# Weight sums of a context-cluster block moved along GpSimd's queue, one half of a norm handed to ScalarE, and the filler pieces of the last batch dealt out anew

## The chip, the cores and the metric

The kernel runs on one core of one Trainium2 chip. A core has TensorE (PE: matmuls, with its weight loads on PEld), VectorE (DVE), ScalarE (ACT), GpSimd (POOL) and the SP queue, which issues most DMAs. Each engine works through its own instructions in the order in which the program issues them. The metric is the device time of one execution in microseconds (us). Before the change the median of three runs is 3128.08 us (3124.45 to 3131.26).

## The reference

Two layers act on x of shape (4, 256, 64, 64), all in float32. The first is full self-attention over the 4096 pixels of an image. The second is a context-cluster block: a norm, two 1x1 convolutions f and v, similarity of every pixel to four centres of its region and head, the best centre taken, sums by centre given back to the pixels, a projection, a residual; then a second norm, an MLP with gelu, another residual, and a scaled pointwise convolution with relus.

```python
q, k, v = (1x1 convolutions of x)                  # q, k: 32 channels, v: 256
x = gamma * softmax(q k) v + x                     # attention, each image
feat, val = conv1x1(gn1(x), f_w, f_b), conv1x1(gn1(x), v_w, v_b)   # 96 channels
sim = sigmoid(beta + alpha * cn . pn)              # unit centres . unit points
sim = sim * one_hot(argmax(sim, axis=centres))
agg = (sim @ v2 + v_cen) / (mask.sum() + 1)
y = x + ls1 * conv1x1(sim.T @ agg, proj_w, proj_b)
hdn = conv1x1(gelu(conv1x1(gn2(y), mlp_w1, mlp_b1)), mlp_w2, mlp_b2)
y = y + ls2 * hdn
z = relu(bn(y * dw_w)); z = relu(bn(conv1x1(z, pw_w)))
```

## The kernel before

The four images are taken one after the other (loop over `b`, L2056). For each there are three stages. **Weighting** (L958) is the attention: 64 units of 4x128 keys by 512 queries, each with score products (L489), the subtraction of the maximum (L655), exponentials (L659 to L661) and the weighted sum (L734). Products of 2x2 blocks are done with seven multiplications instead of eight, so sums of operands have to be made beforehand; GpSimd makes most of them (L664). **Cluster** (L1140) is the first norm, the products of f and v (L1331), the similarities, the choice of the best centre and the projection back. **MLP** (L1634) is the second norm and the MLP, again with seven products, whose weights have to be summed too.

The order of all instructions is written out by hand (`manual_schedule`, L2052), and so is the filling of TensorE's gaps: `fill(n)` (L2044) takes matmuls of a list until their sizes reach n. For the images 0, 1 and 2 the list holds the v, q and k projections of the next image (L443, L351). Image 3 has no next one; its list holds the last 512-pixel block of image 2, which was kept back (`late_block`, L1518). Its pieces are numbered here 0 to 36: 0 to 15 are `first` (L1549), 16 to 31 `second` (L1566; each image column c ends with an ACT instruction L1575, a GpSimd addition L1576, an ACT relu L1577, and after c = 1 a GpSimd subtraction L1586), 32 is empty, 33 to 36 are `last` (L1592, with relus L1600).

What the change touches:

- `turn_mlp` (L248) and `turn_w2` (L1622) make weight sums on GpSimd: L251, L252, L1627, L1629, L1631, each 128x512. For the images 0 to 2 `turn` (L2075) issues all five, for image 3 only the three of `turn_w2`; there `turn_mlp` runs at the end of the weighting (L1087). The cluster stage calls `turn` at L1398, after the choice of the best centres in the program; but on GpSimd's own queue the instruction in front is the last square of `heads` (L1308), so that is what they follow.
- The f and v loop (L1319) runs over eight blocks. Each has 16 matmul records, two additions out of PSUM (L1341), two of the similarities (L1350), a square on GpSimd (`heads`, L1310) and a sum over it on VectorE (L1312). PSUM for it has two buffers (`ps_s`).
- After the loop comes the tail of the choice on VectorE: affine (L1268), `largest` (L1273 to L1281), `weights` (L1286), for two halves in turn, then the sums on TensorE (`summed`, L1366), counts (L1401), transposes (L1412, L1421) and the projection (L1434), then the products with the pixels (L1456).
- `group_norm` (L301) is mean and variance by bn_stats, two matmuls with `left` and `avg` (L309, L310), another (L320), ACT's square root (L224), a reciprocal (L226), and scale and offset (L326, L327). For the second norm it has `meanwhile` load gelu's table right behind the square root. Then `norm(0, nc.vector)` (L1745) applies scale and offset to two channel halves of block 0 (L1667) and makes the sums of it (L1734 to L1737), all on VectorE; the first two hidden products (L1854) need them, and the ACT copy L1862 comes behind the first product.
- At the very start, while no score of the first query block is weighted yet (`alone`, L865), the generator `load_rest` (L176) issues weight loads a part at a time, one part for every u above 2. Its last part is no load but the first sums of `wpw_s` on GpSimd (L188, L189). Behind it on GpSimd stand `added(5)`, `added(6)`, the first `factors` and `added(7)` (L664 all).

Of the kernel before, what the change touches and what calls it, by code (L numbers as in the profile page):

```python
# [10 lines left out]
AF = mybir.ActivationFunctionType  # L11
ALU = mybir.AluOpType
# [48 lines left out]
def attention_then_cluster_block(  # L61
# [17 lines left out]
    nc = tc.nc  # L79
# [168 lines left out]
    def turn_mlp():  # L248

        _, w_cd, _, w_d = own_w["q"]  # L250
        nc.gpsimd.tensor_tensor(w_cd, w_cd, w_d, ALU.add)  # L251
        nc.gpsimd.tensor_scalar(w_d, w_d, -1.0, None, ALU.mult)  # L252

    def roots():
        for s, v in ((dw_d, "dw_v"), (pw_s, "pw_v")):
# [41 lines left out]
    def table(f):  # L297

        nc.scalar.activation(probe, probe, f)
# [30 lines left out]
    def block(tiles, k, nb):  # L330
        o = (nb % 2) * NB
        return tiles[nb // 2][:, k, o : o + NB]
# [5 lines left out]
    def attention(b, xs, ys):  # L338
# [526 lines left out]
        def alone():  # L865

            roots()
            for i in range(2):
                v_pair(i)
            k0, q0 = staged()  # L870
            for i in range(2, 5):
                v_pair(i)

            def added(*gs):
                for g in gs:
                    for f in sums(g):
                        f()

            added(0, 1)
            rest = load_rest()  # L880
            for u in range(GRP):
                half(u, 0)()
                if u < GRP - 1:
                    half(u, 1)()
                else:

                    sc = products(u, 1)
                    highest_of(0, tiles(sc))
                    kept(u, 1, sc)
                if u == 0:  # L890
                    k1 = halved("k", 1, False)
                    for i in range(4, GRP):
                        k_straight(i, k1)
                elif u == 1:
                    q1 = halved("q", 1, False)
                else:
                    v_pair(u + 3)
                    if u % 2 == 0:
                        added(u // 2 + 1)
                if 1 < u < 6:  # L900
                    written("kqkq"[u - 2], (u - 2) // 2, *(k0, q0, k1, q1)[u - 2], nc.gpsimd)
                if u == 3:
                    q_block(1)
                    k_unit(GRP)
                if u > 2:
                    next(rest, None)
            fold(0)
            v_pair(11)
            added(5)
            tp = turned_over(0, ps_m.tile([P, 4, P], F32, tag="m", name=f"tt_{b}_0"))  # L910
            half(GRP, 0)
            v_pair(12)
            dgs["dg"] = across(0, "w2", tp)
            v_pair(13)
            added(6)
            spread(0, dgs["dg"])
            v_pair(14)
            wf()
            exps(0)
            factors(0)  # L920
            v_pair(15)
            half(GRP, 1, True)
            added(7)
            for _ in rest:
                pass
# [32 lines left out]
        def weighting(next_x, fill, early, begin):  # L958
# [23 lines left out]
            for u in range(units):  # L982
                nb, g = divmod(u, GRP)
# [99 lines left out]
            nb = NBLK - 1  # L1083
            for _ in range(4):
                next(quarters)
            if b == B - 1:
                turn_mlp()  # L1087
            table(AF.Sqrt)
            ends = b == B - 1
            fill(1 if ends else 2)  # L1090
# [23 lines left out]
                    stop=True,  # L1114
                )
            nc.scalar.copy(rdens[nb], inv)
            fill(6 if ends else 7)
            t = ts[nb].rearrange("p (h k) n -> p h k n", h=2)
            nc.vector.tensor_tensor(t, t, over(nb), ALU.mult)
            add_one(nb)  # L1120
# [19 lines left out]
    def cluster(b, ys, stats, cells, rest, fill, gelu, nxt, maxima, turn):  # L1140
# [161 lines left out]
        def heads(nb, between=lambda: None):  # L1302
# [13 lines left out]
                ALU.add,  # L1316
            )

        for nb in range(NBLK):  # L1319
            fh, o = nb // 4, nb % 4  # L1320
            if 1 < nb + 1 < NBLK:
                norm(nb + 1)
            if nb in later:
                later[nb]()
            xn = xns.pop(nb)

            ps = ps_s.tile([P, 2, 2, C], F32, tag="s", name=f"fv_{b}_{nb}")
            for j in range(4):
                g = j // 2
                for k in range(KC):  # L1330
                    nc.tensor.matmul(  # L1331
                        ps[:, g, j % 2, : 2 * ED + 16],
                        xn[:, k, j * P : (j + 1) * P],
                        mix[:, k, fh, 16 * g : 16 * g + 2 * ED + 16],
                        start=(k == 0),
                        stop=(k == KC - 1),
                    )
            if nb == NBLK - 1:
                heads(nb - 1)
            for g in range(2):  # L1340
                nc.vector.tensor_tensor(  # L1341
                    vf[nb // 2][:, nb % 2, 2 * g : 2 * g + 2, :],
                    ps[:, g, :, 16 - 16 * g : 16 - 16 * g + 2 * ED],
                    fvb.unsqueeze(1).to_broadcast([P, 2, 2 * ED]),
                    ALU.add,
                )
            for g in range(2):
                q = 2 * fh + g
                d0 = 2 * ED * g
                nc.vector.tensor_tensor(  # L1350
                    folded(sgs[fh])[:, g, 2 * o : 2 * o + 2],
                    ps[:, g, :, d0 : d0 + 16],
                    dot_b[:, q * 16 : (q + 1) * 16].unsqueeze(1).to_broadcast([P, 2, 16]),
                    ALU.add,
                )
            if 0 < nb < NBLK - 1:
                heads(nb - 1)
            if nxt and nb == 2:
                nxt.queries()

        agg_p = ps_a.tile([P, NB], F32, tag="a0", name=f"agg_{b}")

        def summed(w, first):
# [19 lines left out]
        fill(0 if nxt else 2)  # L1383
        summed(lambda j, q: pool_w[:, j], True)
        gelu(1)
        fill(5 if nxt else 4)
        table(AF.Sqrt)
        for _ in best:
            pass
# [5 lines left out]
        summed(lambda j, q: sim[:, j, q, :], False)  # L1395
        count(0)
        count(1)
        turn()  # L1398

        cnt_p = ps_a.tile([P, NB], F32, tag="a1", name=f"cnt_{b}")  # L1400
        nc.tensor.matmul(cnt_p[:ED, :64], ones[:, :ED], bests[0], start=True, stop=True)  # L1401
# [99 lines left out]
        seen(1, 0)  # L1501
        seen(1, 1)
        if not nxt:
            fill(6)
            return stats2

        nxt.q_block(0)
# [111 lines left out]
        t = own_w["w2"]  # L1619
        return t[:, :h_n, :P], t[:, h_n:, :P], t[:, :h_n, P:], t[:, h_n:, P:]  # L1620

    def turn_w2(b, kept):  # L1622


        a11, _, a21, a22 = quarters_w2()
        w7 = work.tile([P, h_n, P], F32, tag="rden", bufs=1, name=f"w2_7_{b}")
        nc.gpsimd.tensor_tensor(w7, a21, a11, ALU.subtract)  # L1627
        s1 = work.tile([P, h_n, P], F32, tag="q", name=f"w2_1_{b}") if kept else a21
        nc.gpsimd.tensor_tensor(s1, a21, a22, ALU.subtract)  # L1629
        s2 = work.tile([P, h_n, P], F32, tag="q", name=f"w2_2_{b}")  # L1630
        nc.gpsimd.tensor_tensor(s2, s1, a11, ALU.subtract)  # L1631
        return s1, s2, w7

    def mlp(b, ys, stats2, fill, nxt, blocks, turned, maxima):  # L1634

# [14 lines left out]
        few = swap.tile([P, h_n + 3, P], F32, tag="mix", name=f"w2_3_{b}")  # L1650
        w3_s, (pw_bcd, pw_bac, pw_abcd) = few[:, :h_n], (few[:, h_n + i] for i in range(3))
        nc.gpsimd.tensor_tensor(w3_s, s2_s, a12_s, ALU.add)
        ga, gb = group_norm(
            b, "gn2", stats2, fill, meanwhile=lambda: table(AF.Gelu_apprx_tanh)
        )
        ob = out[b].rearrange("(k p) h w -> p k (h w)", p=P)
        pairs = {}

# [2 lines left out]
        def norm(nb, eng):  # L1661


            pairs[nb] = pr = spool.tile([P, 2, KC, NB], F32, tag="s", name=f"xn2_{b}_{nb}")

            def scaled(k):
                nc.vector.tensor_scalar(  # L1667
                    pr[:, 0, k, :],
                    block(ys, k, nb),
                    ga[:, k : k + 1],  # L1670
                    gb[:, k : k + 1],
                    ALU.mult,
                    ALU.add,
                )

            def parts():
                rest = factors(eng, pr[:, 0], pr[:, 1])
                scaled(0)
                if nb == 0:
                    next(rest)  # L1680
                scaled(1)
                yield
                yield from rest

            rest = parts()
            next(rest)
            return rest
# [56 lines left out]

        for _ in norm(0, nc.vector):  # L1745
            pass

        def product(out, w, j, x):
            nc.tensor.matmul(out, w[:, j * P : (j + 1) * P], x, start=True, stop=True)
# [302 lines left out]
    with tc.manual_schedule():  # L2052
        here = attention(0, xs0, [])
        here.alone()
        late = None
        for b in range(B):  # L2056
            xs1 = []
            nxt = attention(b + 1, xs1, []) if b + 1 < B else None

            def next_x():  # L2060
                if nxt:
                    xs1.append(load_x(b + 1, len(xs1)))

            begin, todo, gelu = late or (
                lambda: None,
                list(nxt.projections) if nxt else [],
                lambda i: None,
            )
            fill = filler(todo)
            stats, cells, rest = here.weighting(  # L2070
                next_x, fill, [] if b else derived(), begin
            )
            turned = []

            def turn():  # L2075
                if nxt:
                    turn_mlp()
                turned.extend(turn_w2(b, not nxt))

            maxima = []  # L2080
            stats2 = cluster(b, here.ys, stats, cells, rest, fill, gelu, nxt, maxima, turn)

            late = mlp(b, here.ys, stats2, fill, nxt, NBLK - (b == B - 2), turned, maxima)
            here = nxt
# [76 lines left out]
```

## Time and profile before

| | us |
|---|---|
| median of 3 runs | 3128.08 |
| lowest, highest | 3124.45, 3131.26 |
| the profiled execution, whole | 3132.96 |
| its span, first to last instruction | 3131.2 |
| PE busy | 3052.7 (97%) |
| DVE busy | 2513.3 (80%) |
| GpSimd (POOL) busy | 2330.7 (74%) |
| ACT busy | 1780.1 (57%) |
| mean granted TensorE clock | 0.994 |

A line of the timeline reads: start, duration, engine, line of the kernel, operation, output tile <- input tiles, shapes, count, and in brackets the idle time of that engine before it with what ended it. The windows view gives, for each stretch, its length, the busy time of every engine with its number of instructions, the granted TensorE clock (1.00 is full), and the share and rate of the DMA engines. PE's 97% is a mean: in 80 us windows most of the weighting and MLP stages lie at 99% and more, the windows around the cluster stage at 91 to 94% (73.30 of 80 us from 560 to 640, 75.42 from 1280 to 1360, 73.56 from 2080 to 2160, 73.05 from 2880 to 2960).

### The profile page before, as it was taken

Reading aid. Unit: us, or ns where it says so; the run is one execution under the profiler, and the core shown is the slowest. Engines: PE = TensorE matmul, PEld = TensorE weight load, DVE = VectorE, ACT = ScalarE, POOL = GpSimd, SP = SyncE. Lnnn points to the kernel's source line nnn. Section 1 sums busy time; section 2 is a strip of 40 time slices with the busy share of each in tenths; the row PEclk is TensorE's granted clock in tenths of the full one; section 3 lists DMA queues with packets and bytes.
Section 4 is the critical chain, followed back from the end, with each engine's and each line's share of the span. In section 5 each row is a group of like instructions: output and inputs, shape, how many; then the busy total and the mean of one; then the engine's idle time right before and its main releaser. Section 6 shows DMA issues by size and latency. Waiting matters only on the chain.

```text
span 3131.2 us, 41360 instructions
## 1 busy us (share of the span) xinstructions
PE 3052.7 (97%) x14210; PEld 2498.0 (80%) x14210; DVE 2513.3 (80%) x3548; ACT 1780.1 (57%) x2817; POOL 2330.7 (74%) x2243
## 2 busy tenths in 40 slices
PE   8999999999999999999999999999999999999999
PEld 5788887788688888878868888886877888875886
DVE  4999888777798888877779888877768988887675
ACT  5666664544566666454556666645446666655444
POOL 5888886477588888657758888955766988893563
PEclk9999999999999999999999999999999999999999
DMA  5112226100112113510011212440011112150000
GB/s 174 47 56 64 61 90 168 58 18 28 48 47 68 55 61 111 157 44 26 19 58 44 68 61 64 117 144 34 28 41 44 59 57 67 55 153 1 14 21 28
DMA packets 105570, 200.40 MB, mean 64 GB/s; under 512 B 14880, under 2 KB 30864, under 8 KB 103824
## 3 DMA queue, kind: packets, MB, share of 16 engines
q1 hardware_dynamic: 100464, 178.66, 17.9%
q0 software_dynamic: 4256, 18.90, 2.9%
q8 instruction: 113, 1.85, 0.2%
q14 instruction: 97, 0.79, 0.1%
q10 hardware_dynamic: 640, 0.20, 0.0%
HBM read 147.01 MB, written 48.34 MB: 62 GB/s over the span
## 4 chain that ended last, share of the span: by engine, by line
PE 73%; DVE 9%; POOL 9%; issue 3%; ACT 3%; DMA 2%; SPq 1%; POOLq 0%; ACTq 0%; DVEq 0%
PE av L734 34%; PE mo L1771 10%; PE sc L489 7%; PE hq L1854 5%; PE hp L1854 3%; PE hr L1854 3%; PE fv L1331 3%; POOL acc L664 3%; POOL t L664 2%; DVE top L513 2%; DVE s L655 2%; PE vp L443 2%; POOL s L664 1%; PE mo L1755 1%; PE hq_pw L1854 1%
## 5 line engine op out<-in xcount | busy, mean ns | idle before, releaser
L502 ACT COPY s<-sc 128x1024 f32<-128x1024 f32 x512 | 515.2, 1012 | 426.3 <-PE sc L489 418.2
L655 DVE TENSOR_TENSOR s<-s,hold 128x1024 f32<-128x1024 f32 x512 | 598.5, 1209 | 9.9 <-ACT hold L638 6.0
L664 POOL TENSOR_TENSOR acc<-acc,t 128x512 f32<-128x512 f32 x408 | 541.9, 1348 | 0.0
L734 PE MATMUL av<-s,sum 128*128 128x256 f32 x2048 | 527.1, 380 | 5.5 <-POOL s L664 5.3
L734 PE MATMUL av<-t,v 128*128 128x256 f32 x2048 | 527.2, 380 | 2.5 <-POOL t L664 2.4
L734 PE MATMUL av<-s,v 128*128 128x256 f32 x2048 | 525.7, 379 | 2.5 <-ACT t L764 1.3
L664 POOL TENSOR_TENSOR s<-t,s 128x512 f32<-128x512 f32 x256 | 341.9, 1336 | 221.9 <-DVE t L678 154.9
L678 DVE TENSOR_TENSOR t<-s,hold 128x1024 f32<-128x1024 f32 x256 | 311.7, 1217 | 189.4 <-POOL acc L664 98.1
L513 DVE TENSOR_TENSOR top<-sc,top 128x1024 f32<-128x1024 f32 x350 | 426.6, 1219 | 21.4 <-ACT s L502 17.6
L734 PEld LDWEIGHTS av<-s,v 128*128 128x128 f32 x2048 | 387.3, 189 | 65.0 <-ACT xn L1722 2.3
L734 PEld LDWEIGHTS av<-s,sum 128*128 128x128 f32 x2048 | 387.7, 190 | 63.7 <-POOL s L664 11.4
L734 PEld LDWEIGHTS av<-t,v 128*128 128x128 f32 x2048 | 387.4, 190 | 63.4 <-POOL t L664 8.9
L1809 ACT ACTIVATE hs<-hs,pv_s 128x256 f32<-128x256 f32 x496 | 232.6, 503 | 353.2 <-DVE hs L1845 353.2
L489 PE MATMUL sc<-q,k 128*128 128x512 f32 x1024 | 392.8, 468 | 20.0 <-ACT s L502 9.6
L1771 PE MATMUL mo<-hs,w 128*128 128x256 f32 x1512 | 385.0, 381 | 0.0
L664 POOL TENSOR_TENSOR t<-s 128x512 f32<-128x512 f32 x256 | 330.3, 1290 | 45.4 <-PE av L734 31.8
L1771 PEld LDWEIGHTS mo<-hs,w 128*128 128x128 f32 x1512 | 283.7, 190 | 47.3 <-ACT hs L1809 6.2
L659 ACT ACTIVATE hold<-s 128x512 f32<-128x512 f32 x256 | 154.2, 602 | 214.9 <-DVE s L655 214.7
L1845 DVE TENSOR_TENSOR hs<-hq,hs 128x256 f32<-128x256 f32 x496 | 198.5, 421 | 86.6 <-PE hq L1854 76.2
L661 ACT ACTIVATE s<-s 128x1024 f32<-128x1024 f32 x256 | 266.9, 1043 | 0.0
L734 PE MATMUL av<-t,sum 128*128 128x256 f32 x1024 | 262.4, 378 | 0.0
L489 PEld LDWEIGHTS sc<-q,k 128*128 128x128 f32 x1024 | 174.2, 189 | 108.2 <-DVE top L513 59.1
(292 smaller groups left out, 4878.5 us busy)
## 6 DMA issues: line engine op xcount, KB each, us to landing
k<-k SPq DMA_DIRECT2D x248, 256.0 KB, 2.7
x<-in_x SPq DMA_DIRECT2D x62, 512.0 KB, 6.9
out<-xn SPq DMA_DIRECT2D x62, 256.0 KB, 2.1
att<-t SPq DMA_DIRECT2D x56, 256.0 KB, 4.0
x<-att POOLq DMA_DIRECT2D x12, 1024.0 KB, 9.9
w<-in_w SPq DMA_DIRECT2D x8, 1024.0 KB, 11.8
q<-q SPq DMA_DIRECT2D x31, 256.0 KB, 4.1
rden<-row_rd SPq DMA_DIRECT2D x28, 256.0 KB, 3.7
```

The source lines that it names most:

```text
L489: nc.tensor.matmul(sc[:, r, :], k_s[:, (2 * h + r) * P : (2 * h + r + 1) * P], qs[u // GRP], start=True, stop=True,)
L502: nc.scalar.copy(slots[u][:, PAIR[h]].rearrange("p h r n -> p r h n"), tiles(sc))
L513: nc.vector.tensor_tensor(top, src, top if saved[nb] is None else saved[nb], ALU.max)
L655: nc.vector.tensor_tensor(sh, sh, mb.to_broadcast([P, 2, 2, QW]), ALU.subtract)
L661: nc.scalar.activation(s[:, PAIR[1]], s[:, PAIR[1]], AF.Exp)
L664: nc.gpsimd.tensor_tensor(out, x, y, op)
L678: nc.vector.tensor_tensor(t31[u], s[:, B11 : B22 + 1 : 2], b12.to_broadcast([P, 2, 2, QW]), ALU.add)
L734: nc.tensor.matmul(av[bank][:, half_ * QW : (half_ + 1) * QW], a[:, r], t[:, r], start=(g == 0 and r == 0 and i in (1, 7, 2, 4)), stop=(g ...
L1771: return nc.tensor.matmul(bank[:, half * HB : (half + 1) * HB], a[:, j], t, start=start, stop=stop)
L1809: nc.scalar.activation(src, src, AF.Gelu_apprx_tanh, bias=pvc("b1", P, j + 4 * (i > 1)))
L1845: nc.vector.tensor_tensor(dst, ps, term, ALU.add)
L1854: nc.tensor.matmul(out, w, x, start=True, stop=True)
```

## The change

Five edits, none of which changes an operand or a result's formula.

1. `turn_mlp` and `turn_w2` become generators. `turn` is started before the f and v loop, one instruction of it is issued after each `heads(nb - 1)` of the blocks 1 to 6, and what may be left is issued after the loop; the call behind the choice goes.
2. The second norm no longer loads gelu's table behind the square root; the table is loaded after `norm(0)`. In `norm(0)` the second channel half is made by ACT (Identity with scale and offset) instead of VectorE.
3. The `wpw_s` sums of the start are not issued at u = 7; they come with the rest of `load_rest`, behind `added(7)`.
4. In image 3 the pieces of the kept block are handed out otherwise: 8 instead of 6 at the end of the weighting, 6 instead of 4 after gelu(1), 2 instead of 6 after the products with the pixels. So 2 pieces come earlier from there up to the f and v loop, and 4 fewer are left for the wait before the second norm.
5. `turn_mlp` at the end of image 3's weighting is run through at once, as before.

```diff
     def turn_mlp():
         _, w_cd, _, w_d = own_w["q"]
-        nc.gpsimd.tensor_tensor(w_cd, w_cd, w_d, ALU.add)
-        nc.gpsimd.tensor_scalar(w_d, w_d, -1.0, None, ALU.mult)
+        yield nc.gpsimd.tensor_tensor(w_cd, w_cd, w_d, ALU.add)
+        yield nc.gpsimd.tensor_scalar(w_d, w_d, -1.0, None, ALU.mult)
...
-                if u > 2:
-                    next(rest, None)
+                if 2 < u < 7:
+                    next(rest)
...
             if b == B - 1:
-                turn_mlp()
+                for _ in turn_mlp():
+                    pass
...
-            fill(6 if ends else 7)
+            fill(8 if ends else 7)
...
+        turning = turn()
         for nb in range(NBLK):
...
             if 0 < nb < NBLK - 1:
                 heads(nb - 1)
+                next(turning, None)
...
+        for _ in turning:
+            pass
...
-        fill(5 if nxt else 4)
+        fill(5 if nxt else 6)
...
         count(1)
-        turn()
...
         if not nxt:
-            fill(6)
+            fill(2)
             return stats2
...
-    def turn_w2(b, kept):
+    def turn_w2(b, kept, turned):
...
-        nc.gpsimd.tensor_tensor(w7, a21, a11, ALU.subtract)
+        yield nc.gpsimd.tensor_tensor(w7, a21, a11, ALU.subtract)
...
-        nc.gpsimd.tensor_tensor(s1, a21, a22, ALU.subtract)
+        yield nc.gpsimd.tensor_tensor(s1, a21, a22, ALU.subtract)
...
-        nc.gpsimd.tensor_tensor(s2, s1, a11, ALU.subtract)
-        return s1, s2, w7
+        yield nc.gpsimd.tensor_tensor(s2, s1, a11, ALU.subtract)
+        turned.extend((s1, s2, w7))
...
-        ga, gb = group_norm(
-            b, "gn2", stats2, fill, meanwhile=lambda: table(AF.Gelu_apprx_tanh)
-        )
+        ga, gb = group_norm(b, "gn2", stats2, fill)
...
             def scaled(k):
-                nc.vector.tensor_scalar(
-                    pr[:, 0, k, :],
...
-                )
+                dst, src = pr[:, 0, k, :], block(ys, k, nb)
+                a, s = ga[:, k : k + 1], gb[:, k : k + 1]
+                if nb == 0 and k:
+                    nc.scalar.activation(dst, src, AF.Identity, scale=a, bias=s)
+                else:
+                    nc.vector.tensor_scalar(dst, src, a, s, ALU.mult, ALU.add)
...
         for _ in norm(0, nc.vector):
             pass
+        table(AF.Gelu_apprx_tanh)
...
             def turn():
                 if nxt:
-                    turn_mlp()
-                turned.extend(turn_w2(b, not nxt))
+                    yield from turn_mlp()
+                yield from turn_w2(b, not nxt, turned)
```

More of the change, by code (lines that the diff above doesn't have):

```diff
@@ L1666, in scaled @@
             def scaled(k):
-                nc.vector.tensor_scalar(
-                    pr[:, 0, k, :],
[L1669 to L1673, printed above, removed]
-                )
+                dst, src = pr[:, 0, k, :], block(ys, k, nb)
[4 more added lines that the diff above has]
+                    nc.vector.tensor_scalar(dst, src, a, s, ALU.mult, ALU.add)
             def parts():
```

## The prediction

> **What bounds the kernel now.** First the page's chain: which engine holds the end.
>
> ```profile
> PE 73%; DVE 9%; POOL 9%; issue 3%; ACT 3%; DMA 2%; SPq 1%; POOLq 0%; ACTq 0%; DVEq 0%
> ```
>
> TensorE is the bound, and an edit pays only where the chain leaves it. The chain in order of time leaves it in the cluster stage of each image and in the first 90 us. So I read the timeline there; this is image 0 just after f and v:
>
> ```profile
> 565.93 1.33 POOL L251 TENSOR_TENSOR w<-w 128x512 f32<-128x512 f32 x1
> 568.88 1.26 POOL L1627 TENSOR_TENSOR w<-w 128x512 f32<-128x512 f32 x1
> 569.29 1.14 DVE L1281 TENSOR_TENSOR scr<-scr 128x256 f32<-128x256 f32 x1
> 570.22 1.34 POOL L1629 TENSOR_TENSOR w<-w 128x512 f32<-128x512 f32 x1
> 570.46 1.38 DVE L1286 TENSOR_TENSOR sim<-sg,scr 128x256 f32<-128x256 f32 x1
> 571.64 1.32 POOL L1631 TENSOR_TENSOR w<-w 128x512 f32<-128x512 f32 x1
> 571.76 1.49 DVE L1268 TENSOR_SCALAR sg<-sg 128x256 f32<-128x256 f32 x1
> 575.11 0.42 DVE L1281 TENSOR_TENSOR scr<-scr 128x256 f32<-128x256 f32 x1
> 575.57 0.43 DVE L1286 TENSOR_TENSOR sim<-sg,scr 128x256 f32<-128x256 f32 x1
> 576.05 2.78 PE L1366 MATMUL agg<-vf,sim 128*32 128x96 f32 x60 [3.71 <-DVE sim L1286]
> ```
>
> The reader sees the same VectorE instructions twice: beside GpSimd's weight sums each ends 0.2 to 0.3 us after a GpSimd sum ends, and without one it takes a third of that. PE idles 3.71 us behind them. The windows view shows what comes of it (the column before the last two is the granted clock):
>
> ```profile
> 572.00:574.00 2.00, 0.34 (x5) 0.13 (x4) 1.93 (x3) 1.29 (x2) 1.24 (x3) 1.00 0.04 8
> 574.00:576.00 2.00, 0.00 (x0) 0.00 (x0) 1.86 (x6) 0.00 (x0) 0.00 (x0) 0.65 0.00 0
> 576.00:578.00 2.00, 1.95 (x52) 1.95 (x56) 0.98 (x2) 0.00 (x0) 0.00 (x0) 0.50 0.00 0
> 578.00:580.00 2.00, 2.00 (x27) 1.71 (x18) 0.59 (x2) 0.24 (x1) 0.00 (x0) 0.50 0.00 0
> ```
>
> After the gap TensorE runs at half clock. Image 3, where the gap is shorter, does the same sums in 1.51 us at full clock, but loses its clock at another gap, before the first norm:
>
> ```profile
> 2826.00 0.38 PE L309 MATMUL gnm_gn<-mv_gn,left 128*128 128x1 f32 x2 [1.92 <-DVE mv_gn L307]
> 2865.21 0.28 DVE L1268 TENSOR_SCALAR sg<-sg 128x256 f32<-128x256 f32 x1
> 2868.29 1.51 PE L1366 MATMUL agg<-vf,sim 128*32 128x96 f32 x60 [1.41 <-DVE sim L1286]
> ```
>
> At the start GpSimd waits for a weight that nobody needs yet, and VectorE later waits for GpSimd:
>
> ```profile
> 58.62 0.46 POOL L188 TENSOR_TENSOR wpw_s<-wpw_s 128x128 f32<-128x128 f32 x1 [8.05 <-DMA wpw_s<-in_wpw]
> 79.59 1.22 DVE L678 TENSOR_TENSOR t<-s,hold 128x1024 f32<-128x1024 f32 x1 [5.24 <-POOL acc L664]
> ```
>
> **Edit 1, the sums moved into f and v, images 0 to 2.** On the chain L1275 goes from 0.51 to 0.43 us, L1281 from 1.15 to 0.44, L1286 from 1.38 to 0.44, L1268 from 1.42 to 0.21 (0.28 busy less overlap, image 3): -2.94. So the 60 matmuls start at 573.1. PE's last work before ends at 572.35, so 0.76 us of idle time stay, and all 2.94 count. With so short a gap the clock should stay. From these matmuls to the projection (L1434) image 3 takes 2868.29 to 2871.71, 3.42 us at full clock; image 0 took 576.05 to 581.83, 5.78; image 1 1350.34 to 1356.38, 6.04; image 2 2123.18 to 2128.04, 4.86. The clock gives 2.36 + 2.62 + 1.44 = 6.4, the shorter chain 3 x 2.94 = 8.8: **-15.2**. Behind it everything (matmuls, k loads that wait for PE, VectorE's statistics) hangs on PE and moves along.
>
> The cover in the loop: PE needs 2.81 us a block.
>
> ```profile
> 546.53 0.83 POOL L1310 TENSOR_TENSOR vf<-vf 128x384 f32<-128x384 f32 x1 [1.92 <-DVE vf L1341]
> 546.57 0.54 DVE L1312 TENSOR_REDUCE prn<-vf 128x16 f32<-128x384 f32 x1
> ```
>
> GpSimd idles 1.92 to 2.05 us between squares and a sum takes 1.26 to 1.81, so the next square is not late. VectorE's loop work is 1.02 + 0.28 + 0.54 = 1.84 of 2.81. Its additions read PSUM and one tile; a like one, L655, ran its usual 1.2 us beside GpSimd sums, and the row above shows the reduce unharmed by a square. Cost 0; bounds 0 and, if a sum delays an eviction by its whole 1.33, 0.36 a block (1.84 + 1.33 - 2.81) x 13 sums = 4.7. The weights are there: image 1's load lands at 1298, the loop starts at 1314.
>
> By "TensorE: Matmul & The Clock Gate" of the Trainium skill (Part 1) the clock halves after an idle window of about 3.4 us: 0.76 us keeps it, as I assume, but the 1.92 us gap above should have kept it too, and the trace halves it; by the page the 1.35 us claimed below for image 3 would be nothing.
>
> **Edit 3, the start.** GpSimd is idle from 50.57 to 58.62. Freed, `added(5)` (four of 0.81) runs from 52.4, when its v copy is there; `added(6)` waits for the copy ending at 57.17 and ends at 60.4. Then the first s sum waits for L678, at 63.4 instead of 65.94. The rows to `added(7)`'s end took 9.8 us, collisions included; with 1.05 for the moved L188 and L189, the second unit's s sum starts at 74.2 instead of 75.71; one collision less (0.3) makes -1.8. The chain goes on over L678 at 79.59 to PE at 89, and PE has 1.19 + 0.20 + 0.59 + 0.21 + 1.47 + 0.33 = 4.0 us of gaps there. **-1.8**, bounds 0 and -4.0.
>
> **Edit 2, second norm, images 0 to 2.** VectorE sheds L1667, 0.47. But ACT must first copy v out (L451), which waits for PE: in image 1 to 1378.1. An Identity of this shape takes 0.81 (L1529), so L1735 starts at 1378.9 instead of 1378.81; image 0 0.28 later, image 2 0.07: **+0.4**; bounds -1.4 (all of L1667 three times) and +1.7, when L451's 0.57 comes on top each time. Table load and probe (1.28 + 0.20) now stand before the copy L1862: 1380.26 instead of 1380.09, hidden, since the third PSUM bank's user starts after 1381.2.
>
> "ScalarE: Activation LUTs" (What ACT_TABLE_LOAD costs) puts a switch at 2.66 us with its drain; the rows show 1.28 and the probe right behind. By the page L1862 ends 1.4 us late, some 1.2 us beyond that cover, and the sum would be worse by an estimated 3.6.
>
> **Edit 4 and the rest, image 3.** (a) Two pieces of 0.93 fill the 1.92 us before L309 at no cost; the clock then stays, and the three pieces behind take 2.85 instead of 4.20: -1.35. (b) In the tail VectorE sheds 0.07 + 0.49 + 0.99 = 1.55 (L1275, L1261, L1277), but PE has two more pieces: the sums start at 2867.35 instead of 2868.29, -0.94 in all. (c) Piece 30 now ends before the last products. Its L1575, addition L1576 (1.27, after GpSimd is free at 2881.42) and relu (0.81) stand on ACT ahead of the last four L1480, which start at 2884.3 instead of 2882.05: +2.25 up to L307. (d) Four instructions of the norm lost 3.86 to the sums L1647 to L1652 (1.19, 1.58, 1.37, 1.41 instead of 0.23, 0.56, 0.43, 0.47). The sums end near 2899.5 as before, three norm instructions still meet them, the fourth is ACT's. So (c) is eaten up: L1735 starts 0.25 after its old place on the old clock, and with (b) **-0.7**. Bounds: +2.0 if (c) holds whole and (d) gives little; -3.3 if the half clock from 2900.2 to 2906.7 (6.5 us for 3.9) goes too.
>
> **Sum.** -15.2 - 1.8 + 0.4 - 0.7 = -17.3, of the profiled execution's own 3132.96 (span 3131.2): 3115.7. That run lies 4.9 above the median of 3128.08; I take the same gain off the median: **3110.8**.
>
> **Rivals.** *The clock halves anyway* (60 tiny matmuls may not count as work; for it: at 598.5 it halved with PE busy 1.4 of 2; against: image 3 at 2868). Then 6.4 is lost: 3117.2. *VectorE is slow in the tail for another reason* than GpSimd's sums, or is caught by something else: for it, L1273 and L1277 ran at 0.42 beside L251 and L252; against, five slow rows end with a GpSimd sum. Then only -2.1 is left: 3126.0. *Slower*: GpSimd's sums and VectorE's evictions block each other in f and v. A sum then costs its stretched 2.27 (L664 beside L513 at 69.50), and a block 1.84 + 2.27 + 0.83 = 4.94 instead of 2.81: 2.1 x 13 sums = +27.7, net 3138.5. It decides from 1.33 us a sum (17.3 / 13); against it stand the loop's unharmed rows.
>
> **Chances.** Forecast 0.60; clock halves anyway 0.22; tail unchanged 0.12; slower 0.06. About 0.2% (6.3 us) is what a measurement of this kernel can tell from no change. The first two cases and a little of the third are faster by more: 0.84; same 0.10; slower 0.06. Range: the forecast less the bounds of edits 3 and 4 (2.2 + 2.6) and 4 of scatter of the three runs, 3102; up to the second case and 2.7 for edit 4, 3120.
>
> **What shows it.** L1281, L1286, L1268 at 0.45 or less in all images; no gap over 1 us before the 60 matmuls and 1.5 us for them; L1331 at 2.81 a block; L188 behind `added(7)`; image 3's L309 without a gap, but its second mean later than the products ask. Evictions over 1.3 us in f and v, or half clock after them, prove me wrong.

## The result and the profile after

The changed kernel takes 3115.06 us (median of 6 runs, 3113.22 to 3115.55) beside 3128.99 before (6 runs, 3124.45 to 3133.66): a ratio of 0.9954, 95% interval 0.9941 to 0.9967. Faster, as forecast; the forecast time, 3110.8, is 4.3 us too low. The profiled execution takes 3114.76 (span 3113.0, mean granted clock 0.997), so from profile to profile 18.2 us went, where the sum had 17.3.

In what follows a changed kernel's lines are numbered a few higher than before: the 60 matmuls are L1372, `largest` and `weights` L1282 and L1287, `affine` L1269, the sums of `norm(0)` L1735 to L1738, its two halves L1675 (VectorE) and L1673 (ScalarE).

The shares of the page's chain have moved to TensorE:

```profile
PE 75%; DVE 8%; POOL 8%; issue 3%; ACT 3%; DMA 2%; SPq 0%; ACTq 0%; POOLq 0%; DVEq 0%
```

The timeline of image 0, first one block of the f and v loop with the first moved sum, then the tail:

```profile
544.64 1.26 POOL L251 TENSOR_TENSOR w<-w 128x512 f32<-128x512 f32 x1
546.60 0.83 POOL L1311 TENSOR_TENSOR vf<-vf 128x384 f32<-128x384 f32 x1 [0.70 <-DVE vf L1344]
546.63 0.54 DVE L1313 TENSOR_REDUCE prn<-vf 128x16 f32<-128x384 f32 x1
...
569.49 0.42 DVE L1282 TENSOR_TENSOR scr<-scr 128x256 f32<-128x256 f32 x1
569.95 0.43 DVE L1287 TENSOR_TENSOR sim<-sg,scr 128x256 f32<-128x256 f32 x1
570.29 0.29 DVE L1269 TENSOR_SCALAR sg<-sg 128x256 f32<-128x256 f32 x1
...
573.38 1.51 PE L1372 MATMUL agg<-vf,sim 128*32 128x96 f32 x60 [1.00 <-DVE sim L1287]
```

The sum stands in GpSimd's old idle time (0.70 us are left of it), and the next square comes where it came before. In the tail the three instructions that took 1.14, 1.38 and 1.49 us take 0.42, 0.43 and 0.29; TensorE waits 1.00 us instead of 3.71 and does the 60 matmuls in 1.51 us instead of 2.78. The windows view of the same place (the clock is the third column from the end):

```profile
572.00:574.00 2.00, 1.00 (x36) 0.77 (x39) 1.93 (x5) 1.35 (x2) 0.00 (x0) 1.00 0.00 0
574.00:576.00 2.00, 2.00 (x50) 1.69 (x43) 1.04 (x3) 0.55 (x2) 0.00 (x0) 1.00 0.00 0
```

The clock stays at 1.00. Image 3, at both its norms:

```profile
2811.78 0.38 PE L309 MATMUL gnm_gn<-mv_gn,left 128*128 128x1 f32 x2 [0.20 <-DVE mv_gn L307]
...
2867.38 0.81 ACT L1582 ACTIVATE xl<-yl,dw_e,dw_d 128x512 f32<-128x512 f32 x1 [1.38 <-POOL yl L1581]
2868.10 1.82 ACT L1485 ACTIVATE cl<-op,pc_s 128x512 f32<-128x512 f32 x3
2868.84 4.93 POOL L1486 TENSOR_TENSOR x<-cl,x 128x512 f32<-128x512 f32 x4 [1.50 <-ACT cl L1485]
2875.27 0.56 PE L309 MATMUL gnm_gn<-mv_gn,left 128*128 128x1 f32 x2 [8.32 <-DVE mv_gn L307]
2880.64 1.46 DVE L1675 TENSOR_SCALAR xn<-x,ga_gn,gb_gn 128x512 f32<-128x512 f32 x1
```

The first norm's gap is filled (0.20 instead of 1.92 us). Before the second, piece 30's relu (2867.38) stands on ScalarE ahead of the last L1485, GpSimd's last four additions start only at 2868.84, and TensorE idles 8.32 us. The norm's scaling still takes 1.46 us, beside GpSimd's L1652 to L1657.

### The profile page after: what moved, and what is told of

It reads as the page before. It is cut to its first block, busy times and chain, and to the rows that moved or that the text cites. A ratio compares the mean times of both kernels' runs of the same rounds, so it can differ in the third digit from the quotient of the medians.

```text
span 3113.0 us, 41362 instructions
## 1 busy us (share of the span) xinstructions
PE 3042.4 (98%) x14210; PEld 2487.8 (80%) x14210; DVE 2501.1 (80%) x3544; ACT 1782.9 (57%) x2821; POOL 2330.5 (75%) x2243
## 4 chain that ended last, share of the span: by engine, by line
PE 75%; DVE 8%; POOL 8%; issue 3%; ACT 3%; DMA 2%; SPq 0%; ACTq 0%; POOLq 0%; DVEq 0%
PE av L734 35%; PE mo L1773 10%; PE sc L489 7%; PE hq L1856 5%; PE hp L1856 3%; PE hr L1856 3%; PE fv L1334 3%; POOL acc L664 2%; PE vp L443 2%; DVE top L513 2%; POOL t L664 2%; DVE s L655 2%; POOL s L664 1%; PE mo L1757 1%; PE hq_pw L1856 1%
## 5 line engine op out<-in xcount | busy, mean ns | idle before, releaser
L513 DVE TENSOR_TENSOR top<-sc,top 128x1024 f32<-128x1024 f32 x350 | 426.7, 1219 | 22.5 <-ACT s L502 18.6
```

The costliest lines, as they stand in the source:

```text
L513: nc.vector.tensor_tensor(top, src, top if saved[nb] is None else saved[nb], ALU.max)
```

## The experiments

All were timed against the kernel before on the same chip, in three groups: the first four (before: 3130.54, 27 runs), the next four (3129.22, 21 runs), the last three (3131.78, 9 runs).

**Edit 1 alone.**

```diff
 # before, with
+        turning = turn()            # ahead of the f and v loop
...
                 heads(nb - 1)
+                next(turning, None)
...
-        turn()                      # behind the choice
```

> The kernel before with edit 1 alone: GpSimd's weight sums stand inside the f and v loop, the start, the second norm and the pieces are as before. Theory (the sums lengthen VectorE's tail, and the gap behind it costs TensorE its clock): about 5 us in each of the images 0 to 2, as the projection comes 5.0 us earlier behind f and v in image 0 of the changed kernel; -13 to -15 us in the whole, so most of the change's 14. L1281, L1286 and L1268 at 0.45 us or less, the 60 matmuls in 1.5 us. Rival (the gain comes from the other edits): at most -4. Rival (the clock halves anyway): about -8.

3116.75 us, ratio 0.9955 (0.9942 to 0.9967): 13.8 us less, where the whole change gave 13.9. The 60 matmuls take 1.51 us after 1.00 of waiting.

**Edit 1 undone in the changed kernel.**

```diff
                 heads(nb - 1)
-                next(turning, None)
...
-        for _ in turning:               # ahead of the choice
-            pass
...
         count(1)
+        for _ in turning:
+            pass
```

> The changed kernel with edit 1 alone undone: the five weight sums are issued behind the choice again, the other edits stay. Theory: the gain of the images 0 to 2 goes; what stays is image 3's kept clock before the first norm and the like, 1 to 3 us under the kernel before. Rival (edits 2 to 4 make the gain): 10 us or more under the kernel before.

3129.17 us, ratio 1.0000 (0.9991 to 1.0009). The gain is gone with this one edit, and what the others were to leave, 1 to 3 us, can't be told from 0. The 60 matmuls wait 3.71, 3.57 and 3.71 us again and take 2.77, 2.49 and 2.77.

**The clock alone.** The chain and the clock are separated by keeping VectorE slow and TensorE busy.

```diff
         fill(5 if nxt else 4)
+        if nxt:
+            warm = ps_a.tile([P, NB], F32, tag="a1", name=f"warm_{b}")
+            for _ in range(3):
+                nc.tensor.matmul(warm, ident, wpw_s.rearrange("p k m -> p (k m)"),
+                                 start=True, stop=True)
```

> The kernel before, with three more 128x512 matmuls in the images 0 to 2 (identity by wpw_s, into a bank that nobody reads; they add nothing to the result) behind the five pieces ahead of the tail, where TensorE idles 3.71 us. VectorE's tail stays as slow as it was. Theory (the gap costs the clock): the 60 matmuls start where they did but take 1.5 us instead of 2.8 at full clock, -6.4 us over the three images in an execution that lost its clock in all of them (2.36 + 2.62 + 1.44), and single runs lie closer together than before's 9.2 us, since executions that lose and keep the clock no longer differ. Rival (the clock halves whatever TensorE does, or takes no time): 0, within 1.5 us.

3124.14 us, ratio 0.9980 (0.9971 to 0.9989): 6.4 us less, while VectorE's tail is as slow as before. The timeline of image 0:

```profile
571.52 1.49 DVE L1268 TENSOR_SCALAR sg<-sg 128x256 f32<-128x256 f32 x1
571.60 2.74 PE L1390 MATMUL warm<-wpw_s,ident 128*128 128x512 f32 x6
575.81 1.51 PE L1366 MATMUL agg<-vf,sim 128*32 128x96 f32 x60 [1.18 <-DVE sim L1286]
```

L1268 takes its 1.49 us, and the 60 matmuls start where they did (576.05 before), but take 1.51 us instead of 2.78; the windows view has the clock at 1.00 from 570 to 580. The time from the first f and v matmul to the second norm's mean splits the gain of edit 1:

| us | image 0 | image 1 | image 2 | sum |
|---|---|---|---|---|
| before | 60.32 | 60.19 | 59.01 | 179.52 |
| three more matmuls | 57.83 | 57.81 | 57.81 | 173.45 |
| edit 1 alone | 55.07 | 55.07 | 55.06 | 165.20 |
| changed | 55.07 | 55.08 | 55.08 | 165.23 |

The clock makes 6.1 of it, the shorter chain 8.2. The single runs spread over 5.9 us (3122.52 to 3128.43, 11 runs; the kernel before over 8.1 in 27): closer together, as expected, but these three gaps are not the whole of the scatter.

**Edit 3 alone.**

```diff
-                if u > 2:
-                    next(rest, None)
+                if 2 < u < 7:
+                    next(rest)
```

> The kernel before with edit 3 alone: the first sums of wpw_s behind added(7). The prediction gave -1.8 us. Theory from the changed kernel's trace: TensorE is itself 0.6 us later there behind the k load, the moved sum meets VectorE's L513, and the half microsecond that is left at 90 us is gone by 246 us, where another wait (the row maximum and its DMA) ends last; so 0, within 1 us, in the whole.

3129.59 us, ratio 0.9997 (0.9988 to 1.0006): nothing that can be told from 0, though 1.8 lies within the interval.

**Edit 2 alone.**

```diff
+                if nb == 0 and k:
+                    nc.scalar.activation(dst, src, AF.Identity, scale=a, bias=s)
...
         for _ in norm(0, nc.vector):
             pass
+        table(AF.Gelu_apprx_tanh)
```

> The kernel before with edit 2 alone: the second half of the second norm on ScalarE, gelu's table behind it. The prediction gave +0.4 us for the images 0 to 2; in image 3 one of the four norm instructions that met GpSimd's sums leaves VectorE, up to -1.4. Theory: from the second norm's first mean to the first hidden product 5.4 us as before in the images 0 to 2, so 0, within 1.5 us, in the whole. Rival (the later table load delays the copies behind the first products): +3 or more.

3130.00 us, ratio 1.0005 (0.9996 to 1.0014). In image 0 the second hidden product comes 5.46 us after the mean's matmul (598.90 to 604.36). No cost of 3 us from the later table load.

**Edit 4 alone.**

```diff
-            fill(6 if ends else 7)
+            fill(8 if ends else 7)
...
-        fill(5 if nxt else 4)
+        fill(5 if nxt else 6)
...
-            fill(6)
+            fill(2)
```

> The kernel before with edit 4 alone: image 3's pieces dealt out otherwise. Theory: about -3 us where image 3's first norm keeps its clock (1.7 us earlier from the first norm to f and v, and 1.35 us of clock), and +1.5 to +2.3 us back before the second norm, where ScalarE does piece 30's tail ahead of the last products: -1, within 1.5 us. Rival (piece 30 in front costs nothing): -3. Rival (GpSimd's weight sums still in the tail eat the gain): 0 or above.

3128.27 us, ratio 0.9995 (0.9986 to 1.0004): 1 us less, as expected, but the interval holds the numbers of both rivals too. From the first norm's mean to the first hidden product of image 3 it takes 70.69 us (2824.54 to 2895.23). With the old dealing and the clock kept (edit 3 alone) it is 69.24 (2824.94 to 2894.18), although two pieces of 0.93 more stand in that stretch there: what fills the first gap is lost again before the second norm, as the theory had it.

**Pieces 30 and 31 behind the last products.**

```diff
-        fill(2)
+        fill(2 if nxt else 1)
         products(single(1, 1, 0), single(1, 1, 1), *pair(1, 1, 2))
...
-            fill(2)
+            fill(3)
```

> The changed kernel with pieces 30 and 31 both behind the last products of image 3 (1 piece instead of 2 between the second and third group of products, 3 instead of 2 behind them). Theory (piece 30's addition and relu stand on ScalarE ahead of the last L1485, and GpSimd's last additions wait for those): the last L1454 ends by VectorE's own work near 2873.3 instead of 2874.5 us, so the second norm comes 1 to 1.5 us earlier, and the whole is 1 to 1.5 us under the changed kernel. Rival (the norm waits for the products, not for piece 30): 0.

3113.39 us, ratio 0.9950 (0.9937 to 0.9962). The last additions start earlier, and the mean with them:

```profile
2864.30 4.95 POOL L1486 TENSOR_TENSOR x<-cl,x 128x512 f32<-128x512 f32 x4 [0.53 <-ACT cl L1485]
2872.31 0.56 PE L309 MATMUL gnm_gn<-mv_gn,left 128*128 128x1 f32 x2 [6.02 <-DVE mv_gn L307]
```

TensorE idles 6.02 us instead of 8.32. From the sums with `sim` to the mean it is 21.69 us (2850.62 to 2872.31) instead of 23.13: 1.44 less, so piece 30 was in the way. In the whole the intervals don't tell it from the changed kernel.

**That gap filled as well.**

```diff
             fill(3)
+            warm = ps_s.tile([P, 2, NB], F32, tag="s", name=f"warm_{b}")
+            for i in range(7):
+                nc.tensor.matmul(warm[:, i % 2, :], ident, wpw_s..., start=True, stop=True)
```

> The kernel of the two pieces last, and behind them seven more 128x512 matmuls in image 3 (identity by wpw_s, into a bank that nobody reads; they add nothing to the result), so that TensorE does not idle 8.3 us before the second norm's mean. Theory (that gap alone costs the clock there): the matmuls of the mean and of the last pieces run at full clock, 0.28 and 0.47 us instead of 0.56 and 0.94, and the first hidden product comes 1 to 2 us earlier than without them. Rival (VectorE's and GpSimd's collisions end last there, not TensorE): 0 against the kernel of two pieces last.

3112.86 us, ratio 0.9948 (0.9935 to 0.9960): 0.5 less than without. The mean's matmul takes 0.35 instead of 0.56 us, but VectorE gives it back:

```profile
2877.73 1.57 DVE L1684 TENSOR_SCALAR xn<-x,ga_gn,gb_gn 128x512 f32<-128x512 f32 x1
2879.33 1.37 DVE L1744 TENSOR_TENSOR xn<-xn 128x256 f32<-128x256 f32 x1
```

Both stand beside GpSimd's weight sums (L1662 to L1666). The rival holds here.

**The changed kernel again**, as the measure for the last two.

> The changed kernel once more, unaltered, on the chip of the two runs beside it, as what they are measured against: 13 to 15 us under the kernel before.

3115.14 us (3111.38 to 3115.74), ratio 0.9945 (0.9931 to 0.9958): 16.6 us less this time.

**Image 3's other four sums into the loop too.** The kernel is that with the two pieces last; the MLP stage of image 3 no longer makes these four sums, and block 1 of the loop issues two.

```diff
+        if kept:
+            ... # four slices t of a tile in v's buffer
+            yield nc.gpsimd.tensor_tensor(t[0], W_CD, W_A, ALU.subtract)
+            yield nc.gpsimd.tensor_tensor(t[1], t[0], W_D, ALU.add)
+            yield nc.gpsimd.tensor_tensor(t[2], W_B, t[0], ALU.subtract)
+            yield nc.gpsimd.tensor_tensor(turned[-1], s2, quarters_w2()[1], ALU.add)
```

> The kernel of the two pieces last, with edit 1's thought carried on in image 3: the four further weight sums (w_abcd, w_bac, w_bcd, w3), which met VectorE's second norm, are also made in the f and v loop, into the buffer of v, which nobody needs any more. Theory (GpSimd's sums are what makes L327, L1675 and L1735 take 1.30, 1.46 and 1.37 us): they take 0.23, 0.47 and 0.43, the second hidden product comes 2 to 3 us earlier, and the whole is 3.5 to 5 us under the changed kernel. Rival (TensorE's last pieces at half clock, up to 2878.5 us, end last): 1 us or less beyond the kernel of the two pieces last. Rival (four more sums are too many for the loop): f and v longer than 22.9 us, and slower.

3110.29 us (3109.59 to 3112.48), ratio 0.9933 (0.9920 to 0.9945): 4.9 under the changed kernel beside it. The f and v matmuls of image 3 take 22.67 us as with three sums, so seven are not too many. In the second norm TensorE is late next:

```profile
2878.05 3.76 PE L1599 MATMUL pwl<-xl,wpw_s 128*128 128x512 f32 x4
2878.99 0.22 DVE L327 SCALAR_TENSOR_TENSOR gb_gn<-ga_gn,dv_gn,pc_s 128x2 f32<-128x2 f32 x1
2879.24 0.55 DVE L1690 TENSOR_SCALAR xn<-x,ga_gn,gb_gn 128x512 f32<-128x512 f32 x1
2881.61 0.94 PE L1871 MATMUL hp<-xn,w 128*128 128x256 f32 x2
```

L327 takes 0.22 instead of 1.30, the scaling 0.55 instead of 1.46; its result is there at 2879.8, but TensorE does its last pieces at half clock until 2881.6.

**Both.** The seven matmuls in front of the same norm.

```diff
             fill(3)
+            ... # the seven matmuls shown above
```

> The kernel before this one with the seven matmuls that add nothing to the result in image 3's gap ahead of the second norm, so that TensorE keeps its clock there. Theory (with the collisions gone TensorE's half clock is late next): 1 to 2 us less than without them. Rival (ScalarE's copy of the second half ends last): 0, within 0.5 us.

3107.63 us (3106.27 to 3109.74), ratio 0.9924 (0.9911 to 0.9936): 7.5 under the changed kernel, with no run in common, and the fastest here.

```profile
2874.00 1.98 PE L1608 MATMUL pwl<-xl,wpw_s 128*128 128x512 f32 x4 [0.20 <-ACT xl L1593]
2875.61 0.55 DVE L1699 TENSOR_SCALAR xn<-x,ga_gn,gb_gn 128x512 f32<-128x512 f32 x1
2876.21 0.70 PE L1880 MATMUL hp<-xn,w 128*128 128x256 f32 x2 [0.22 <-DVE xn L1699]
```

From the second mean to the second hidden product, which waits for the first factor, the four kernels of image 3 take 9.25 us (pieces last), 8.94 (gap filled), 7.30 (sums moved) and 5.05 (both). Alone the edits give 0.3 and 2.0, together 4.2: each hides behind the other.

## Why the prediction was right, and where it was off

**Edit 1 (-15.2).** Right in mechanism and nearly in size: 14.3 by the table, 8.2 for the chain (8.8 said) and 6.1 for the clock (6.4). The chain gave 2.74 us up to the 60 matmuls in image 0 (36.55 us from the start of f and v before, 33.81 after), not 2.94, and 1.00 us of idle time stayed instead of 0.76. That the sums cost nothing in the loop held: f and v take 8.71 and 14.33 us for the same two runs of matmuls before and after. The rival "the clock halves anyway" fell with the clock of 1.00, "tail slow for another reason" with the tail's rows and with edit 1 undone, the slower case with f and v, whose 64 additions out of PSUM take 0.55 to 0.56 us each before and after. Two readings in the sum were wrong, without harm: the projections L1434 start at 581.67, 1356.19 and 2127.88, which makes the clock's term 5.9, and the loop makes 18 sums (five in each of the images 0 to 2, three in image 3), not 13.

By "SBUF — State Buffer" of the Trainium skill (Who interferes with whom) a VectorE instruction with two SBUF inputs waits for a GpSimd instruction that reads SBUF until that ends, while a reduce, or an addition with one input in PSUM, does not. The runs agree for L1282 (0.42 against 1.14), the reduce L1313 (0.54 in both) and L1344 out of PSUM (1.02 for two in both). They do not agree everywhere. Before the change, L252, which reads one tensor, runs from 567.36 to 568.90, and inside that time L1261 and L1277, each with two inputs in SBUF, are not slowed:

```profile
568.38 0.42 DVE L1277 TENSOR_TENSOR scr<-scr,rank 128x256 f32<-128x256 f32 x1
```

The prediction had noted this for its rival; why L252 does no harm there is open. In image 3, beside L1629 and L1631, which read two tensors, the same two instructions take 0.91 and 1.49. And L1268, the largest single loss (1.49 beside L1631, 0.28 alone), has one input in SBUF, so the sentence cited does not cover it.

**Edit 3 (-1.8).** This term was too large. A score product of TensorE starts 0.52 us earlier at 89 us (88.56 against 89.08), and another still 0.58 us earlier at 229 us (229.43 against 230.01). Both executions have a gap of 2.02 us there; behind it the changed kernel's ran at half clock (0.50 from 230 to 232), the other's at 1.00, and f and v of image 0 start at 539.57 against 539.50. So what was left of the gain went with a lost clock, and not with another wait, which the theory of the run with edit 3 alone had named. Two steps of the sum were wrong. The moved sum met VectorE's L513, and TensorE was itself later, behind the k load:

```profile
53.01 0.71 PE L489 MATMUL sc<-q,k 128*128 128x512 f32 x2 [0.37 <-DMA k<-k]
73.03 1.55 POOL L188 TENSOR_TENSOR wpw_s<-wpw_s 128x128 f32<-128x128 f32 x1
```

The s sum starts at 64.11, not 63.4, and L188 takes 1.55 us beside L513, not 0.46. The later k load is not the edit's doing: over the 13 profiled executions this product starts anywhere from 52.40 to 55.42, with and without edit 3, and the kernel before had the earliest. Counted from it, the second unit's s sum comes after 23.31 us before and after 22.19 in the changed kernel. But four kernels without edit 3, whose k came later, need only 22.03 to 23.04 (edits 1, 2 and 4 alone, three more matmuls). The step that fell is that GpSimd's wait decides: in these profiles it does so in full only where k landed early.

**Edit 2 (+0.4).** Too small to be told: 0.8 (interval -1.3 to +4.4) alone; from the mean to the second hidden product image 1 takes 5.46 us after and 5.40 before.

**Edit 4 and image 3 (-0.7).** The mechanisms (a) and (c) were right, the sizes were not. From the first norm's mean to f and v it took 9.21 us before and 7.52 after, so (a) is worth 1.69, not 1.35. With (b) the 60 matmuls came 1.83 us sooner after that mean (42.29 us before, 40.46 after), not 0.94. Piece 30 in front cost 1.35 us from these matmuls to the second mean (21.68 before, 23.03 after), not 2.25; 1.44 us were to be had back. Profile to profile image 3 gave 3.9 us (1.6 up to f and v, 2.3 behind), more than the bound of 3.3. Behind f and v the second mean came 1.2 us later, the way from it to the second hidden product was 1.3 us shorter (10.24 before, 8.91 after), and no half clock followed: from that product to the next block's first it took 6.3 us before (2900.21 to 2906.53) and 3.7 after (2884.18 to 2887.91). Of these 2.7 us 0.4 went again further on. Edit 4 alone brings nothing that can be measured.

**The sum and the median.** The errors of -1.8 and -0.7 went opposite ways, and that 17.3 came close to 18.2 was in part luck. The step that made the forecast 4.3 us too low is "I take the same gain off the median". Taken from the profiled execution's own time the sum gives 3115.7, within a microsecond of the 3115.06 measured. That execution had itself lost more clock than most: its stage of the table above takes 179.5 us, where it is unchanged otherwise 178.5 (edit 3 alone), 178.3 (edit 2 alone), 178.1 (edit 1 undone) and 177.9 (edit 4 alone), and its image 3 lost 1.69 us at the first norm, which edit 3 alone did not. Against the profiled execution of edit 3 alone (3130.02) these two make 2.7 of the 2.9 us that it is slower. All 63 runs of the kernel before have the median 3129.97, and the 11 of the changed one 3115.11: 14.9 us between them. The gain is what an execution had lost, and the profiled one had more to lose.

## What to carry to other kernels

GpSimd work that fitted into its idle time cost nothing here beside VectorE instructions that read PSUM or reduce, and sums of two tensors on GpSimd cost much beside VectorE's sums and scalings that read only SBUF: place such work by what VectorE does then, not only by when its result is needed. Two limits that hide each other (VectorE's collisions and TensorE's clock) show their worth only when both are taken away. A gain that rests on a lost clock belongs to the execution in which it was lost: subtract it there, and look at other executions before moving it to a median.

## What the runs showed of the hardware that was not expected

The same gap costs the clock in some executions and not in others, in steps. The timeline of edit 3 alone, then of edit 1 alone, both with the old dealing of image 3's pieces:

```profile
2824.94 0.38 PE L309 MATMUL gnm_gn<-mv_gn,left 128*128 128x1 f32 x2 [1.92 <-DVE mv_gn L307]
2825.41 1.10 PE L1549 MATMUL hlp<-xl,w 128*128 128x512 f32 x2
```

```profile
2810.77 0.38 PE L309 MATMUL gnm_gn<-mv_gn,left 128*128 128x1 f32 x2 [1.91 <-DVE mv_gn L307]
2811.42 2.06 PE L1553 MATMUL hlp<-xl,w 128*128 128x512 f32 x2
```

The two matmuls behind take 1.10 us here and 2.06 there. After 1.91 to 1.92 us of waiting the stretch from the mean to f and v takes 7.52 us (edit 3 alone, three more matmuls), 9.20 (before, edit 2 alone) or 10.89 (edit 1 alone): 0, 1.7 or 3.4 us lost. In the traces' record of the granted clock the half clock there lasts 3.41 us where 1.7 were lost, and 6.83 where 3.4 were. "TensorE: Matmul & The Clock Gate" of the Trainium skill (Part 1) has activity judged in windows of about 3.4 us that run freely, and the steps agree with one and two such windows. Its condition, a whole idle window, does not agree: 1.9 us were enough in three of these five executions.

Counted over all 13 profiled executions: gaps of 1.41 to 1.47 us never cost the clock (17 gaps), gaps of 1.91 to 2.05 us did in 6 of 18, and gaps of 3.44 to 3.71 us always did (20). Matmuls into a bank that nobody reads kept it, in the images 0 to 2 (1.00 from 570 to 580) and in image 3's gap before the second norm (1.00 from 2866 to 2878 in the run with that gap filled).
